# PSUM as one tile of eight banks, minima of the first heads one by one, and VectorE's attention work in program order, in a transformer block

## The chip, the cores and the metric

The kernel runs on one core of a Trainium2 chip. The metric is the device time of one execution in microseconds (us). Three executions took 3985.17, 3985.71 and 3986.91 us; the median is 3985.71 us. The engines are called PE (TensorE, matrix multiplications), ACT (ScalarE), DVE (VectorE), POOL (GpSimd) and SP (SyncE). PSUM is the accumulator memory that PE writes and that ACT and DVE read. Here it has 128 partitions and eight banks, each of 512 float32 numbers per partition.

## What is computed

Both parts work on h of shape (8, 1024, 512): causal attention with 16 heads of width 32, and a feed-forward part of width 2048. Each normalises its input, and its result is normalised again and added to the input.

```python
# attention, for x = layernorm(h)
qvk = (x @ Wqvk).reshape(b, s, 3, H, HD)
scores = einsum('bshi,bthi->bsth', q, k)
scores = (scores + mask) / sqrt(d)
...
h = h + layernorm(attention(layernorm(h)))
# feed-forward, for x = layernorm(h)
hidden = x @ W1 + b1
imag   = w_imag * sin(theta + hidden * 0.1)
hidden = hidden + (cos(theta) * w_real + sin(theta) * w_imag) * imag * 0.1
y = relu(hidden) @ W2 + b2
out = h + layernorm(y)
```

The lines above are a summary of the reference in its own names. All matmuls are in float32. In the trace each float32 matmul of 512 columns shows as two records.

## The kernel before

**The work and its order.** The kernel takes the eight batches one after the other. A batch has attention, in four groups of four heads (`attention`, L631), and then the feed-forward part (`feed_forward`, L743). Every PE instruction is pinned to program order: the helper `matmul` (L88) and `transpose_on_pe` (L94) call `keep_in_program_order`. Much of ACT's work is pinned too, through `in_order` (L91). DVE's instructions are not pinned, and a scheduler chooses their order before the program is built. Functions that are written as generators (`project_qkv`, `norm1`, `finish_block`) are advanced step by step between the other stages, so that their matmuls stand among those of the attention. SP issues the loads and stores.

**PSUM.** `psum` (L78) gives out four slots of up to two banks, s0 to s3, each with a tag of its own. `drained` (L84) puts a slot back at the end of a list, and the next request takes the one at its head. So a request for one bank takes a slot of two. Requests are: `pq` and `pv` (projections, one bank or half of one), `sc` (scores, two banks), `parts_t` (transposed maxima), `st` (transposed scores, two banks), `acc` (the weighted values in its first bank and, in the second half of the queries, the sums of weights in its second), `y` (output projection), `xn_t` (transposes of the normalised input), `ph` (two chunks of the hidden layer, one bank each) and `ys` (four row blocks of the result in two tiles of two).

**A group of heads.** `find_maxima` (L419) works through four runs, in the order of `MAX_RUNS` (L403). A run has one or two units. A unit (`run_unit`, L447) takes two tiles `sc`, one for heads 0 and 1 and one for heads 2 and 3, multiplies queries by keys for all four heads into them, and lets DVE take minima of each row (the sign is turned). Where a block of keys is visible as a whole, one `tensor_reduce` (L471) covers the two heads of a tile. On the diagonal a masking operation (L478) runs for each head, and leaves `es`, which ACT turns into exponentials (L497). After each run `MAX_FILL` (L412) steps of the next group's projections follow: `pq` (L359) with its copy L372, and `pv` (L377) with its copy L388. The maxima are split into parts (L431), transposed on PE (`transpose_maxima`, L528) and copied to `mT` (L533), by ACT for the first half of the queries and by DVE for the second.

`weigh` (L537) then runs for three units of keys in the first half and seven in the second (`KEY_UNITS`, L414). It fills two tiles `st`, ACT turns each into weights `w` (L573), and POOL cuts off what the mask hides (L577). The next unit's scores are issued ahead of the weighted values (`weighted_values`, L590) of this one. In the second half `add_weights` (L616, the addition is L621) sums the weights on DVE, `weight_sums` (L603) multiplies the total by ones, and `divide` (L623) has a logarithm, an exponential and a product (L626 to L628). These sums are put off into the first run of the next group. Two last units of maxima, `MAX_LATE`, run between the units of weights.

**The feed-forward part.** `hidden` (L752) takes a chunk of 128 hidden columns: four multiplications into one bank of `ph`, then ACT's `hid` (L770), then DVE's chain and ACT's sine. `accumulate` (L784) adds the chunk of two steps before into `ys`. A `ph` tile serves two chunks and is drained after the second. Between them stand steps of `finish_block` (L711): `y` with its copy L728, the residual addition (`residual_stages`, L259, the function `add`), and the transposes into `x2T` (L237). `end` (L797) reads `ys` with four additions (L802). `norm1` (L330) does the same for the input of the next batch, with its `scale` at L341 (`normalised`, L218).

Of the kernel before, what the change touches and what calls it, by code (L numbers as in the profile page):

```python
# [16 lines left out]
P = 128  # L17
# [14 lines left out]
def kernel(  # L32
# [42 lines left out]
    free_slots = list(range(4))  # L75
    slot_of = {}

    def psum(shape, name, dtype=F32):  # L78
        slot = free_slots.pop(0)
        t = ps.tile(shape, dtype, tag=f"s{slot}", name=name)  # L80
        slot_of[id(t)] = slot, t
        return t

    def drained(t):  # L84

        free_slots.append(slot_of.pop(id(t))[0])

    def matmul(*args, **kwargs):  # L88
        tc.keep_in_program_order(nc.tensor.matmul(*args, **kwargs))  # L89
# [90 lines left out]
    def prepare_parameters():  # L180

        pt = psum([P, 4 * NFC], "prm_t")
        transpose_on_pe(pt, prm_in, ident[: 4 * NFC, : 4 * NFC])
        nc.vector.tensor_copy(prm, pt)
        drained(pt)
        th, wr, wi = (prm[:, n * NFC : (n + 1) * NFC] for n in (1, 2, 3))
        sn = small.tile([P, NFC], F32, tag="sn", name="sn", bufs=1)
        cs = small.tile([P, NFC], F32, tag="cs", name="cs", bufs=1)
        kk = small.tile([P, NFC], F32, tag="kk", name="kk", bufs=2)
        reduce_angle(sn, kk, th, 0.0)  # L190
        clamp(sn)
        nc.scalar.activation(sn, sn, AF.Sin)
        kc = small.tile([P, NFC], F32, tag="kk", name="kc", bufs=2)
        reduce_angle(cs, kc, th, 0.25)
        nc.vector.tensor_scalar(cs, cs, math.pi / 2, None, ALU.add)
        clamp(cs)
        nc.scalar.activation(cs, cs, AF.Sin)
        nc.vector.tensor_mul(cs, cs, wr)
        nc.vector.tensor_mul(sn, sn, wi)
        nc.vector.tensor_add(cs, cs, sn)  # L200
        nc.vector.scalar_tensor_tensor(coef, cs, 0.1, wi, ALU.mult, ALU.mult)
# [16 lines left out]
    def normalised(dst, src, mv, rs):  # L218
        nc.vector.tensor_scalar(dst, src, mv[:, 0, 0:1], rs, ALU.subtract, ALU.mult)
# [13 lines left out]
    def transpose_rows(src, dst, evacuate):  # L233
        pt = psum([P, KC, P], "xn_t")
        for kc in range(KC):
            transpose_on_pe(pt[:, kc, :], src[:, kc * P : (kc + 1) * P], ident)
        evacuate(dst, pt)  # L237
        drained(pt)
# [20 lines left out]
    def residual_stages(target, y):  # L259
# [8 lines left out]
        def add(t):  # L268
            normalised(y(t), y(t), mvs[t], rss[t])
            nc.vector.tensor_add(target(t), target(t), y(t))  # L270
# [59 lines left out]
    def norm1(b):  # L330
# [10 lines left out]
        def scale(t):  # L341
            normalised(xs[t], xs[t], mvs[:, t : t + 1, :], rss[:, t : t + 1])
# [7 lines left out]
    def project_qkv(b, g):  # L350
# [7 lines left out]
        def queries_or_keys(n, half):  # L358
            pq = psum([P, HALF], "pq")  # L359
            c0 = 2 * n * D + g * P  # L360
            for kc in range(KC):
                matmul(
                    pq,
                    wqvk_sb[:, kc, c0 : c0 + P],
                    xnT[b, half][:, kc, :],
                    start=(kc == 0),
                    stop=(kc == KC - 1),
                )
                if kc == 1:
                    yield True  # L370
# [5 lines left out]
        def values(t0):  # L376
            pv = psum([P, 2, P], "pv")  # L377
            c0 = D + g * P
            for t in (t0, t0 + 1):
                for kc in range(KC):  # L380
                    matmul(
                        pv[:, t - t0, :],
                        xnT[b, t // TPB][:, kc, (t % TPB) * P : (t % TPB + 1) * P],
                        wqvk_sb[:, kc, c0 : c0 + P],
                        start=(kc == 0),
                        stop=(kc == KC - 1),
# [32 lines left out]
    def find_maxima(b, g, work, sums):  # L419
# [11 lines left out]
        def split(c):  # L431
# [6 lines left out]
            else:  # L438
                nc.vector.tensor_tensor(top, top, mxs[c][:, 1], ALU.min)
            parts = parts_q[c].rearrange("p i (j r) -> p i j r", r=HD)  # L440
            engine, keep = (nc.vector, id) if c else (nc.gpsimd, tc.keep_in_program_order)
            for r in range(MPART):
                keep(engine.tensor_copy(parts[:, :, :, r], top))
                if r < MPART - 1:
                    keep(engine.tensor_tensor(top, top, parts[:, :, :, r], ALU.subtract))

        def run_unit(pieces):  # L447

            scs = [psum([P, 2, HALF], "sc") for _ in range(HC)]
            at = 0  # L450
            placed, left = [], []
            for i, kc in pieces:
                k0 = kc * HALF
                n = min(HALF, (i + 1) * P - k0)
                for j in range(HPG):
                    r = slice(j * HD, (j + 1) * HD)
                    matmul(
                        scs[j // 2][:, j % 2, at : at + n],
                        t[r, 0, i * P : (i + 1) * P],
                        t[r, 1, k0 : k0 + n],  # L460
                        start=True,
                        stop=True,
# [3 lines left out]
            for k, sc in enumerate(scs):  # L466
                es = None
                for i, kc, cols, n in placed:
                    mx = mxs[i // TPB][:, kc, i % TPB, 2 * k : 2 * k + 2]
                    if kc < i // TPB:  # L470
                        nc.vector.tensor_reduce(  # L471
                            out=mx, in_=sc[:, :, cols], op=ALU.min, axis=mybir.AxisListType.X
                        )
# [3 lines left out]
                    for m in range(2):  # L477
                        nc.vector.tensor_tensor_reduce(  # L478
                            out=es[:, m, cols],
                            in0=sc[:, m, cols],  # L480
                            in1=mask[:, HALF - n :],
                            scale=1.0,
                            scalar=FMAX,
                            op0=ALU.add,
                            op1=ALU.min,
                            accum_out=mx[:, m : m + 1],
# [41 lines left out]
    def transpose_maxima(parts, evacuate):  # L528
        pt = psum([P, TPB, P], "parts_t", BF16)
# [7 lines left out]
    def weigh(b, g, c, keys, mT):  # L537
# [3 lines left out]
        sts = [psum([P, 2, HALF], "st") for _ in range(HC)]  # L541
        at = 0
        placed, own = [], []
        for kb in keys:
# [3 lines left out]
            for j in range(HPG):  # L548
                r = slice(j * HD, (j + 1) * HD)
                matmul(  # L550
                    sts[j // 2][:, j % 2, cols],
                    minus1[r, :],
                    mT[r, HALF - n :],
                    start=True,
                    stop=False,
                )
            for j in range(HPG):
                r = slice(j * HD, (j + 1) * HD)
                matmul(
                    sts[j // 2][:, j % 2, cols],  # L560
                    t[r, 1, kb * P : (kb + 1) * P],
                    t[r, 0, q0 : q0 + n],
                    start=False,
                    stop=True,
# [25 lines left out]
    def weighted_values(acc, b, g, first, last, weights, placed):  # L590

        for k, (kb, cols, n) in enumerate(placed):
            for j in range(HPG):
                r = slice(j * HD, (j + 1) * HD)
                matmul(
                    acc[r, 0, HALF - n :],
                    v[b, g][:, kb, r],
                    weights[j // 2][:, j % 2, cols],
                    start=first and k == 0,
                    stop=last and k == len(placed) - 1,  # L600
                )

    def weight_sums(acc, first, last, weights, placed):  # L603

        for k, (_, cols, n) in enumerate(placed):
            for j in range(HPG):
                r = slice(j * HD, (j + 1) * HD)
                matmul(
                    acc[r, 1, HALF - n :],
                    ones,  # L610
                    weights[j // 2][:, j % 2, cols],
                    start=first and k == 0,
                    stop=last and k == len(placed) - 1,
                )

    def add_weights(total, weights, placed):  # L616

        for t, w in zip(total, weights):
            for _, cols, n in placed:
                q = slice(HALF - n, HALF)  # L620
                nc.vector.tensor_add(t[:, :, q], t[:, :, q], w[:, :, cols])  # L621

    def divide(acc, dst):  # L623

        inverse = tmp.tile([P, HALF], F32, tag="tmp", name="inverse")
        in_order(nc.scalar.activation(inverse, acc[:, 1, :], AF.Ln))  # L626
        in_order(nc.scalar.activation(inverse, inverse, AF.Exp, scale=-1.0))
        nc.vector.tensor_tensor(dst, acc[:, 0, :], inverse, ALU.mult)  # L628
        drained(acc)

    def attention(b, wvT, after):  # L631
# [23 lines left out]
        for g in range(NG):  # L655
# [4 lines left out]
            for c in range(2):  # L660
# [3 lines left out]
                for u, keys in enumerate(units):  # L664
# [4 lines left out]
                    if at == 2:  # L669
                        mTs.append(transpose_maxima(parts_q[1], nc.vector.tensor_copy))  # L670
# [13 lines left out]
                    def step(accs=accs, u=u, last=u == len(units) - 1, weights=weights, c=c, g=g,  # L684
                             placed=placed, total=total, dst=wvT[c][:, g, :]):
                        if u == 0:
                            accs.append(psum([P, 1 + c, HALF], "acc"))
                        acc = accs[0]
                        weighted_values(acc, b, g, u == 0, last, weights, placed)
                        if last and c:  # L690

                            def whole():
                                weight_sums(acc, True, True, *total)
                                divide(acc, dst)

                            summing[0] = whole
                        elif last:
                            nc.scalar.copy(dst, acc[:, 0, :])
# [12 lines left out]
    def finish_block(b, half, wvT, x2T):  # L711
# [5 lines left out]
        def project(t):  # L717
            y = psum([P, D], "y")
            for kc in range(KC):
                matmul(  # L720
                    y,
                    wvT[:, kc, t * P : (t + 1) * P],
                    wo_sb[:, kc, :],
                    start=(kc == 0),
                    stop=(kc == KC - 1),
# [17 lines left out]
    def feed_forward(b, x2T, between):  # L743
# [6 lines left out]
        ys, hids, phs, us, ks = {}, {}, {}, {}, {}  # L750

        def hidden(c):  # L752

            half, fc = divmod(c, NFC)
            n, pair = c % 2, c // 2
            if n == 0:
                phs[pair] = psum([P, 2, HALF], "ph")
# [3 lines left out]
            ph, hid, u, k = (x[pair][:, n, :] for x in (phs, hids, us, ks))  # L761
            for kc in range(KC):
                matmul(
                    ph,
                    w1_sb[:, kc, fc * P : (fc + 1) * P],
                    x2T[half][:, kc, :],
                    start=(kc == 0),
                    stop=(kc == KC - 1),
                )
            nc.scalar.activation(hid, ph, AF.Identity, bias=prm[:, fc : fc + 1])  # L770
            if n:
                drained(phs[pair])
# [11 lines left out]
        def accumulate(c):  # L784
            half, fc = divmod(c, NFC)
            for t in range(TPB):
                if fc == 0 and t % 2 == 0:
                    ys[half, t // 2] = psum([P, 2, D], "ys")
                matmul(
                    ys[half, t // 2][:, t % 2, :],  # L790
                    hids[c // 2][:, c % 2, t * P : (t + 1) * P],
                    w2_sb[:, fc, :] if fc < NW2 else w2_tail[:, fc - NW2, :],
                    start=(fc == 0),
                    stop=(fc == NFC - 1),
                )

        def end(half):  # L797

            ybs = []
            for t in range(TPB):  # L800
                yb = tmp.tile([P, D], F32, tag="tmp", name="yb")
                nc.vector.tensor_add(yb, ys[half, t // 2][:, t % 2, :], b2_sb)  # L802
                if t % 2:
                    drained(ys[half, t // 2])
# [101 lines left out]
```

## Time and profile before

| | us |
|---|---|
| median of three executions | 3985.71 |
| the profiled execution's own time | 3986.48 |
| its span in the trace | 3984.8 |
| PE busy | 3826.0 (96% of the span) |
| DVE busy | 2767.8 (69%) |
| ACT busy | 1503.3 (38%) |
| POOL busy | 515.8 (13%) |
| mean granted clock of PE | 0.998 of full speed |

The profile comes from one execution. The page lists busy times, the granted clock of PE and the costliest groups of instructions; a group's row gives the line, the engine, the operation, the tiles written and read, the count, the busy time, the mean of one, and the idle time ahead of it with the instruction that ended most of it. A row of waits such as `PE pq L89 <- DVE mx L471` says that PE sat idle ahead of matmuls into `pq`, and that the last event before they started was the end of a minimum on DVE at line 471; three numbers follow, the sum in us, the number of times, and the longest. All matmuls are recorded at line 89, so they are told apart by the tile that they write. In the timeline each row has its start, its length, what it is, and in brackets the idle time before it with its releaser. A batch takes 492.6 us; its feed-forward part takes about 238.

### The profile page before, as it was taken

The page shows a single profiled execution, that of the slowest core. Times are in us where ns is not written, and L with a number is a line of the kernel's source. Part 1 is how long each engine was busy: PE and PEld are TensorE (multiplying, and loading weights), DVE is VectorE, ACT ScalarE, POOL GpSimd, SP SyncE. Part 2 cuts the span into 40 slices and gives each one's busy share as a digit, 9 for nine tenths or more (in the row PEclk, how much of TensorE's full clock was granted, in tenths as well). Part 3 has the DMA queues.
Part 4 walks back from the last instruction along what each step waited for, and adds up shares of the span by engine and source line. Part 5 has one row for each costly group of instructions (what it writes and reads, how often), then busy time and mean ns, then how long its engine had stood idle before and what let it go on. Part 6 is the DMA issues. An engine that isn't in the chain of part 4 may idle for free.

```text
span 3984.8 us, 51177 instructions
## 1 busy us (share of the span) xinstructions
PE 3826.0 (96%) x19457; PEld 1756.0 (44%) x19457; DVE 2767.8 (69%) x6033; ACT 1503.3 (38%) x2804; POOL 515.8 (13%) x1131
## 2 busy tenths in 40 slices
PE   8999999999999999999999999999999999999998
PEld 4444444444444444444444444444444444444343
DVE  4767767676766777667776677766767666677666
ACT  4552135521354214542145421454214542146321
POOL 1121011200112001120011200111001110011200
PEclk9999999999999999999999999999999999999999
DMA  4000000000000000000000000000000000000000
GB/s 151 25 19 22 22 30 9 17 21 21 30 14 12 22 21 32 12 12 21 22 32 12 12 21 21 33 12 11 22 22 33 12 11 0 22 22 12 1 8 14
DMA packets 43495, 86.42 MB, mean 22 GB/s; under 512 B 4144, under 2 KB 4208, under 8 KB 42736
## 3 DMA queue, kind: packets, MB, share of 16 engines
q1 hardware_dynamic: 39056, 71.61, 5.4%
q10 hardware_dynamic: 4192, 11.53, 0.7%
q8 instruction: 152, 2.49, 0.2%
q14 instruction: 95, 0.78, 0.1%
HBM read 66.36 MB, written 16.78 MB: 21 GB/s over the span
## 4 chain that ended last, share of the span: by engine, by line
PE 83%; DVE 10%; ACT 2%; issue 2%; POOL 1%; DMA 0%; POOLq 0%; ACTq 0%; SPq 0%
PE ph L89 22%; PE ys L89 22%; PE pq L89 11%; PE st L89 6%; PE pv L89 6%; PE acc L89 6%; PE sc L89 5%; PE y L89 4%; DVE mx L471 4%; ACT w L573 2%; DVE es L478 2%; DVE w L621 1%; DVE st L207 1%; PE xn_t L95 1%; DVE x L270 1%
## 5 line engine op out<-in xcount | busy, mean ns | idle before, releaser
L89 PE MATMUL ph<-x2T,w_sb 128*128 128x512 f32 x2048 | 921.1, 593 | 12.1 <-ACT hid L770 6.7
L89 PE MATMUL ys<-w_sb,hid 128*128 128x512 f32 x1536 | 691.0, 592 | 0.0
L573 ACT ACTIVATE w<-st 128x1024 f32<-128x1024 f32 (+1 forms) x640 | 565.8, 936 | 295.8 <-PE st L89 288.2
L89 PEld LDWEIGHTS ph<-x2T,w_sb 128*128 128x128 f32 x2048 | 385.3, 190 | 487.5 <-issue 466.8
L621 DVE TENSOR_TENSOR w<-w 128x1024 f32<-128x1024 f32 (+3 forms) x448 | 443.2, 1033 | 161.0 <-PE acc L89 108.0
L478 DVE CUSTOM_DVE_ANT_0 es<-sc,mask 128x128 f32<-128x128 f32 (+3 forms) x1024 | 433.5, 487 | 149.3 <-PE sc L89 149.3
L89 PE MATMUL pq<-xnT,wqvk_sb 128*128 128x512 f32 x1024 | 480.9, 609 | 43.0 <-DVE mx L471 43.0
L778 ACT ACTIVATE u<-u 128x512 f32<-128x512 f32 x256 | 161.1, 629 | 891.0 <-DVE u L178 890.9
L89 PEld LDWEIGHTS ys<-w_sb,hid 128*128 128x128 f32 x1536 | 291.2, 190 | 368.6 <-issue 344.2
L471 DVE TENSOR_REDUCE mx<-sc 128x2 f32<-128x1024 f32 x256 | 302.2, 1220 | 145.6 <-PE sc L89 145.6
L577 POOL TENSOR_SCALAR_AFFINE_SELECT w<-w 128x256 f32<-128x256 f32 x512 | 263.7, 534 | 729.4 <-ACT w L573 724.4
L89 PE MATMUL acc<-w,v 128*32 128x512 f32 (+3 forms) x3072 | 323.8, 495 | 25.0 <-POOL w L577 16.8
L770 ACT ACTIVATE hid<-ph,prm 128x512 f32<-128x512 f32 x256 | 175.2, 685 | 451.8 <-PE ph L89 451.8
L89 PE MATMUL st<-qk 32*128 32x512 f32 (+3 forms) x3072 | 334.7, 494 | 0.0
L89 PE MATMUL sc<-qk 32*128 32x512 f32 (+3 forms) x3072 | 312.8, 511 | 3.3 <-DVE mx L478 3.1
L781 DVE SCALAR_TENSOR_TENSOR hid<-u,coef,hid 128x512 f32<-128x512 f32 x256 | 192.2, 751 | 173.5 <-ACT u L778 173.5
L773 DVE TENSOR_SCALAR u<-hid,prm 128x512 f32<-128x512 f32 x256 | 123.8, 484 | 270.9 <-ACT hid L770 270.9
L89 PEld LDWEIGHTS pq<-xnT,wqvk_sb 128*128 128x128 f32 x1024 | 182.8, 190 | 289.8 <-issue 182.4
L497 ACT ACTIVATE es<-es,mx 128x512 f32<-128x512 f32 (+3 forms) x512 | 279.6, 550 | 1.9 <-DVE mx L478 1.9
L89 PE MATMUL pv<-wqvk_sb,xnT 128*128 128x128 f32 x2048 | 259.5, 280 | 13.5 <-DVE mx L478 13.5
L89 PEld LDWEIGHTS pv<-wqvk_sb,xnT 128*128 128x128 f32 x2048 | 239.0, 192 | 75.4 <-DVE mx L478 40.8
L89 PE MATMUL y<-wo_sb,wvT 128*128 128x512 f32 x512 | 233.5, 599 | 0.0
(96 smaller groups left out, 3380.1 us busy)
## 6 DMA issues: line engine op xcount, KB each, us to landing
xin<-in_L_attn_h_dram SPq DMA_DIRECT2D x112, 256.0 KB, 2.6
x<-in_L_attn_h_dram SPq DMA_DIRECT2D x64, 256.0 KB, 2.7
out_dram<-x SPq DMA_DIRECT2D x64, 256.0 KB, 2.0
w_tail<-in_L_ffn_W_dram SPq DMA_DIRECT2D x8, 1024.0 KB, 5.2
w_sb<-in_L_ffn_W_dram ACTq DMA_DIRECT2D x1, 4096.0 KB, 15.8
wqvk_sb<-in_L_attn_Wqvk_dram ACTq DMA_DIRECT2D x3, 1024.0 KB, 9.5
w_sb<-in_L_ffn_W_dram ACTq DMA_DIRECT2D x1, 3072.0 KB, 25.1
wo_sb<-in_L_attn_Wo_dram ACTq DMA_DIRECT2D x1, 1024.0 KB, 5.5
```

Source lines behind the costliest of these rows:

```text
L89: tc.keep_in_program_order(nc.tensor.matmul(*args, **kwargs))
L95: tc.keep_in_program_order(nc.tensor.transpose(*args))
L471: nc.vector.tensor_reduce(out=mx, in_=sc[:, :, cols], op=ALU.min, axis=mybir.AxisListType.X)
L478: nc.vector.tensor_tensor_reduce(out=es[:, m, cols], in0=sc[:, m, cols], in1=mask[:, HALF - n :], scale=1.0, scalar=FMAX, op0=ALU.add, op1 ...
L497: nc.scalar.activation(es[:, m, cols], es[:, m, cols], AF.Exp, bias=mx[:, m : m + 1], scale=-1.0, accum_out=row[:, m : m + 1],)
L573: in_order(nc.scalar.activation(w[:, :, :width], st[:, :, :width], AF.Exp, scale=-1.0))
L577: select = nc.gpsimd.affine_select(out=square, in_=square, compare_op=ALU.is_ge, fill=0.0, base=0, pattern=[[0, 2], [1, P]], channel_multi ...
L621: nc.vector.tensor_add(t[:, :, q], t[:, :, q], w[:, :, cols])
L770: nc.scalar.activation(hid, ph, AF.Identity, bias=prm[:, fc : fc + 1])
L773: nc.vector.tensor_scalar(u, hid, 0.1, prm[:, NFC + fc : NFC + fc + 1], ALU.mult, ALU.add)
L778: sine = nc.scalar.activation(u, u, AF.Sin)
L781: nc.vector.scalar_tensor_tensor(hid, u, coef[:, fc : fc + 1], hid, ALU.mult, ALU.add)
```

## The change

The change has three parts, and a change of form.

1. PSUM becomes one tile `banks` of eight banks. `psum` gives out one bank, or two neighbouring ones, as a view of this tile: among the free places it takes the one whose last bank to be drained was drained longest ago in program order. `drained` can mark one bank of a pair. Requests that need one bank get one: `pq`, `pv`, `y`, `ph`, `ys`, `xn_t`, `parts_t`, the parameters, and `acc`. The sums of the weights get a bank of their own, `whole_sum`, which is drained after the logarithm. Only `sc` and `st` ask for pairs.
2. In a unit with full keys the minimum of the first tile (k = 0) is taken head by head, with two reductions in place of one. The second tile keeps one reduction for two heads.
3. DVE's work in attention is pinned to program order: the minima, the split of the maxima, the copy of `mT`, the additions of weights, the product of the division, the residual additions and the scaling in `norm1`. The casts and the chain in `hidden`, the moments and the additions in `end` are not pinned.
4. The helper `matmul` goes, and its calls are written as `in_order(nc.tensor.matmul(...))`. PE's order stays the program's.

The core of the diff:

```diff
-    free_slots = list(range(4))
-    slot_of = {}
-
-    def psum(shape, name, dtype=F32):
-        slot = free_slots.pop(0)
-        t = ps.tile(shape, dtype, tag=f"s{slot}", name=name)
-        slot_of[id(t)] = slot, t
+    banks = ps.tile([P, 8, HALF], F32, name="banks")
+    done_at = [0] * 8
+    clock = [0]
+    banks_of = {}
+
+    def psum(shape, dtype=F32):
+        size = math.prod(shape[1:]) * (2 if dtype == BF16 else 4)
+        n = -(-size // (4 * HALF))
+        free = [k for k in range(9 - n) if None not in done_at[k : k + n]]
+        k = min(free, key=lambda k: max(done_at[k : k + n]))
+        t = banks[:, k : k + n, :].rearrange("p b n -> p (b n)")[:, : size // 4]
...
+        done_at[k : k + n] = [None] * n
+        banks_of[id(t)] = list(range(k, k + n)), t
         return t
-    def drained(t):
-
-        free_slots.append(slot_of.pop(id(t))[0])
+    def drained(t, n=None):
+
+        mine = banks_of[id(t)][0]
+        for k in [mine[0]] if n is None and len(mine) == 1 else mine if n is None else [mine[n]]:
+            clock[0] += 1
+            done_at[k] = clock[0]
...
         def add(t):
-            normalised(y(t), y(t), mvs[t], rss[t])
-            nc.vector.tensor_add(target(t), target(t), y(t))
+            in_order(normalised(y(t), y(t), mvs[t], rss[t]))
+            in_order(nc.vector.tensor_add(target(t), target(t), y(t)))
...
-            scs = [psum([P, 2, HALF], "sc") for _ in range(HC)]
+            scs = [psum([P, 2, HALF]) for _ in range(HC)]
...
                     if kc < i // TPB:
-                        nc.vector.tensor_reduce(
-                            out=mx, in_=sc[:, :, cols], op=ALU.min, axis=mybir.AxisListType.X
-                        )
+
+                        for m in [slice(0, 2)] if k else [slice(0, 1), slice(1, 2)]:
+                            in_order(
+                                nc.vector.tensor_reduce(
+                                    out=mx[:, m],
+                                    in_=sc[:, m, cols],
+                                    op=ALU.min,
+                                    axis=mybir.AxisListType.X,
+                                )
+                            )
                         continue
...
-                nc.vector.tensor_add(t[:, :, q], t[:, :, q], w[:, :, cols])
+                in_order(nc.vector.tensor_add(t[:, :, q], t[:, :, q], w[:, :, cols]))
...
-    def divide(acc, dst):
+    def divide(acc, total, dst):
 
         inverse = tmp.tile([P, HALF], F32, tag="tmp", name="inverse")
-        in_order(nc.scalar.activation(inverse, acc[:, 1, :], AF.Ln))
+        in_order(nc.scalar.activation(inverse, total, AF.Ln))
+        drained(total)
         in_order(nc.scalar.activation(inverse, inverse, AF.Exp, scale=-1.0))
-        nc.vector.tensor_tensor(dst, acc[:, 0, :], inverse, ALU.mult)
+        in_order(nc.vector.tensor_tensor(dst, acc, inverse, ALU.mult))
         drained(acc)
...
-                        mTs.append(transpose_maxima(parts_q[1], nc.vector.tensor_copy))
+                        mTs.append(
+                            transpose_maxima(
+                                parts_q[1], lambda *a: in_order(nc.vector.tensor_copy(*a))
+                            )
+                        )
...
-                            accs.append(psum([P, 1 + c, HALF], "acc"))
+                            accs.append(psum([P, HALF]))
...
-                                weight_sums(acc, True, True, *total)
-                                divide(acc, dst)
+                                whole_sum = psum([P, HALF])
+                                weight_sums(whole_sum, *total)
+                                divide(acc, whole_sum, dst)
...
+            ph = psum([P, HALF])
             if n == 0:
-                phs[pair] = psum([P, 2, HALF], "ph")
...
             nc.scalar.activation(hid, ph, AF.Identity, bias=prm[:, fc : fc + 1])
-            if n:
-                drained(phs[pair])
+            drained(ph)
...
-                if fc == 0 and t % 2 == 0:
-                    ys[half, t // 2] = psum([P, 2, D], "ys")
+                if fc == 0:
+                    ys[half, t] = psum([P, D])
```

## The prediction

> **What bounds the kernel now.** I read the table of busy time first, then what TensorE (PE) waits for, then the timeline of single spots, then the granted clock.
>
> ```profile
> PE 3826.0 (96%) x19457; PEld 1756.0 (44%) x19457; DVE 2767.8 (69%) x6033; ACT 1503.3 (38%) x2804; POOL 515.8 (13%) x1131
> ```
>
> PE is busy for 96% of the span, so the kernel is a stream of matmuls, and every other engine lies beside it. What is left over is in PE's waits (us in total, times, longest):
>
> ```profile
> PE pq L89 <- DVE mx L471: 43.0, 86, 2.8
> PE xn_t L95 <- DVE xn L219: 18.8, 9, 17.2
> PE acc L89 <- POOL w L577: 16.8, 26, 1.0
> PE pv L89 <- DVE mx L478: 13.5, 31, 0.4
> PE st L89 <- DVE mT L533: 12.3, 7, 1.8
> ...
> PE acc L89 <- DVE mx L471: 8.2, 31, 0.3
> PE ph L89 <- ACT hid L770: 6.7, 8, 0.8
> ```
>
> The rows of the whole view, without the start-up row xn_t, sum to 124.9 us, 15.6 per batch. That is all a better handing out of PSUM could win. The row that decides my forecast is the last: `ph` waits eight times, once per batch, for ScalarE's (ACT's) read `hid`. Here is one of the eight:
>
> ```profile
> 1783.94 1.02 PE L89 MATMUL ph<-x2T,w_sb 128*128 128x512 f32 x2
> 1785.07 0.69 ACT L770 ACTIVATE hid<-ph,prm 128x512 f32<-128x512 f32 x1 [3.32 <-PE ph L89]
> ...
> 1785.81 1.12 PE L89 MATMUL ph<-x2T,w_sb 128*128 128x512 f32 x2 [0.84 <-ACT hid L770]
> ```
>
> The matmuls at 1783.94 are the last of chunk 0, into the first bank of a two-bank tile. Those at 1785.81 are the first of chunk 1, into the *second* bank, which nobody has touched. They need nothing of `hid`, yet they start when its read of the *first* bank ends. So in this program a write into one bank of a PSUM tile waits for the earlier read of another bank of the same tile: waits go by tile, not by bank. In the steady state nothing shows, because work on another tile stands between:
>
> ```profile
> 1799.72 3.60 PE L89 MATMUL ph<-x2T,w_sb 128*128 128x512 f32 x8
> 1803.15 3.60 PE L89 MATMUL ys<-w_sb,hid 128*128 128x512 f32 x8
> ```
>
> In this stretch ACT reads `ph` from 1803.35 for 0.69 us, beside `ys`. The four slots of L78 are four tiles, and that lets PE write one while another is read.
>
> **The change part by part.** *One tile of eight banks.* With waits by tile, everything in PSUM is one object: a matmul into any bank waits for each read traced before it, and each read waits for the matmuls traced before it. PE and the readers then take turns. The price of a turn is read from the spot above. The matmuls of chunk 0 start 0.43 apart, so the next was due at 1784.80; it started at 1785.81, and that pair took 1.12 instead of 1.02 us. The loss is 1.01 + 0.10 = 1.11 us: the reader's 0.69 plus **0.42** for the two handovers. (Bounds of the 0.42: nothing, if the handovers are hidden elsewhere, and 0.84, the whole idle time of that row, which would add 182 turns x 0.42 x 8 = 611 us to what follows.)
>
> Readers per group of four heads (32 groups), from the groups of instructions:
> - causal minima L478: 433.5/32 = 13.5 us, in 5 units of scores
> - full-key minima L471: 302.2/32 = 9.4, in 4 units, plus the split of the next part, 0.6
> - exponentials of the weights L573: 565.8/32 = 17.7, in 10 units
> - copies of queries and keys L372, 76.4/32 = 2.4 in 4; of values L388, 47.6/32 = 1.5 in 4; transposed maxima L533, 0.58 + 0.42 = 1.0 in 2; first half's result L698, 0.6 in 1
> - the division, L626, L627, L628 one after another: 0.60 + 0.63 + 0.69 = 1.9 in 1
>
> This is 48.6 us and 31 turns: 48.6 + 31 x 0.42 = 61.6 per group, 246.5 per batch. Per batch there are also 8 transposes of the next input (0.59 + 0.42: 8.1), 8 output projections and 8 transposes behind them (0.58 + 0.42: 16.0), 32 hidden chunks (0.69 + 0.42: 35.5) and 8 reads of `ys` in two rows (8 x 0.68 + 2 x 0.42: 6.3). The sum is 312.4 per batch. Today's 15.6 of idle are waits of the same kind and go into it: 296.8 more. Times 8 is 2374; the last batch has no next input and no projections for it, -15. **Added: about 2360 us**, on 3986.5 us (the profiled execution's own time, 0.8 above the median shown): 6346. With turns at nothing it is (312.4 - 182 turns x 0.42 - 15.6) x 8 = 1763, so 5750.
>
> *The clock.* PE would now pause some 31 times per group. The granted clock in before already falls at sparse places:
>
> ```profile
> 3676.42:3679.84 3.42, 2.89 (x20) 1.24 (x20) 3.42 (x7) 2.31 (x8) 0.00 (x0) 1.00 0.00 0
> 3679.84:3683.25 3.41, 2.27 (x20) 1.12 (x20) 3.41 (x17) 2.40 (x9) 0.22 (x1) 1.00 0.00 0
> 3683.25:3686.67 3.42, 2.71 (x16) 1.27 (x12) 3.42 (x15) 0.59 (x1) 1.21 (x5) 0.50 0.00 0
> 3686.67:3690.08 3.41, 3.41 (x20) 1.78 (x18) 3.39 (x12) 0.09 (x1) 0.00 (x0) 0.50 0.02 5
> ```
>
> (The second column is PE's busy time, the third from the end the clock.) After a stretch of 3.41 us with PE busy for 2.27, the next ran at 0.50, although other stretches with 1.66 to 2.20 were not followed by one. Serialized, a group is about 53.4 us of PE work in some 111, so 1.64 of 3.41. All of the attention at half clock would add its PE work once more, 53.4 x 32 = 1709 us; none adds nothing. I take a third, since the rows show both answers: **+570**, in all **6900**. The feed-forward part stays dense (two times 3.43 us of matmuls for every 1.11 us lost).
> [...]
> [...]
>
> *Single banks, and who gets them.* The sums of weights get their own bank, `ph`, `ys` and the accumulator one each, and the least recently drained bank is given. Under waits by tile this moves nothing: which bank is given doesn't matter.
>
> *First heads one by one.* 128 pair reductions of 1.22 us become 256 of half the width. A half isn't in the trace: it takes from 0.61 (half the pair) to 0.69 (a 512-wide pass, L207), so the split costs 0 to 0.16 each, 0 to 20 us of VectorE in all. I take 0.16 (the row of the same width). Beside PE it is hidden by VectorE's 31% of idle time; in turns it is on the path, and is in the sum.
>
> *VectorE in program order.* The instructions and their count stay. What goes: the copy of the transposed maxima (L533) that today stands behind a residual addition is traced ahead of it, so the 12.3 us row goes in 7 batches. What could come: minima queued behind additions of weights (L621, 1.03 us each, two per unit). Under turns these run while ACT reads and PE writes, so I cost both at nothing beyond the sum; without that cover it would be 14 additions per group, up to 14.4 x 32 = 461 us, which the upper end takes in. The scalar and GpSimd work is not moved, nor any DMA.
>
> **Rivals.**
> *Waits by bank, and the change does what it seems to be built for.* The pq row (43.0), pv (13.5), acc behind minima (8.2), mT (12.3) and st behind `xnT` (3.2) go: -80, **3906**. For it: in these rows a projection that needs one bank waits for a slot of two, both banks of which must be read first. Against it: the `ph` row.
> *Waits by bank, but pairs are broken up by singles.* Single banks for `pq` leave no free adjacent pair but the one just read. By the grant rule the second unit of the third run gets the banks of the same run's first heads and waits about 1.1 us, and the first weights get the banks of the late minima (0.9, a third unit 0.15); two pq waits of 0.45 go: +1.25 per group, 5.0 per batch, less 1.5 for the mT row: +28, **4014**. It decides where the single bank lies inside the oldest pair.
> *Faster than forecast but still in turns.* Handovers at nothing and no half clock: 5750.
> For the forecast the other side is the first rival: one mechanism (a guard by bank), worth 80 us, deciding as soon as a write to one bank doesn't wait for another bank's read.
>
> **How the numbers follow.** Waits by tile, in turns: 0.88, since all eight places of this kind in the trace show it. Waits by bank with the gain: 0.05, faster. Broken pairs: 0.05, slower. Between the two, within 0.2% (about what a measurement of this kernel can tell from no change): 0.02. The range for the turns goes from 5800 (5750 with cheap handovers, a little clock loss) to 8000 (6346 and 1709 of clock are 8055; with queued additions still more); I give what lies outside 0.07. So 5800 to 8000 holds about 8 in 10. Slower 0.93, same 0.02, faster 0.05.
>
> **What would show it.** In the changed profile PE's share falls to near 60%; the waits name rows like ys behind ACT `hid`, some 30 per batch, and pq behind any reader, each about the reader's time plus 0.3; ACT and VectorE wait for PE in turn; windows of attention show 0.50 clocks. Feed-forward takes about 280 us per batch instead of 238, attention over 500 instead of 255. Wrong it is if ys starts while `hid` still reads, with `ph` in another bank: then a rival holds, and the time is below 4050. Only the clock is wrong if all stretches show 1.00 and the time is near 6350.

## The result and the profile after

The changed kernel takes **4028.21 us** (median of four executions, 4027.42 to 4028.94), against 3986.31 us for the kernel before on the same chip: a ratio of 1.0104, 95% interval 1.0086 to 1.0121. It is 1% slower, the forecast was 6900 us, and of the rivals the one with broken pairs (4014) is the nearest. The profiled execution has a span of 4026.5 us against 3984.8 of before, 41.7 more.

The table of busy time of the changed kernel:

```profile
PE 3889.7 (97%) x19457; PEld 1780.9 (44%) x19457; DVE 2791.0 (69%) x6161; ACT 1508.6 (37%) x2804; POOL 545.7 (14%) x1131
```

PE's share did not fall; PE is busy for 63.7 us *more* than before, with the same matmuls. PE's waits in the changed kernel (all of PSUM is one tile, so all are called `banks`, and the lines tell them apart: 373 is `pq`, 394 `pv`, 472 `sc`, 576 and 587 `st`, 625 the weighted values, 640 the sums of weights, 805 `ph`, 832 `ys`):

```profile
PE banks L576 <- DVE mx L502: 21.1, 46, 0.6
PE banks L625 <- POOL w L606: 18.0, 34, 0.7
PE banks L472 <- DVE mx L490: 17.6, 38, 3.4
...
PE banks L640 <- DVE w L654: 11.4, 7, 1.6
PE banks L576 <- ACT w L602: 9.2, 40, 0.5
PE banks L832 <- DVE hid L824: 9.0, 8, 1.1
PE banks L576 <- DVE mx L490: 8.8, 25, 0.4
```

Set against the rows of before: pq (43.0), pv (13.5), mT (12.3) and acc behind minima (8.2) are gone, as the first rival said. The row of `ph` behind `hid` (6.7) is gone too, and with it my forecast: `ph` no longer waits for a read of another bank. In the steady state `ys` starts while `hid` still reads `ph` in another bank of the same tile, which was my sign of being wrong:

```profile
1824.42 3.60 PE L832 MATMUL banks<-w_sb,hid 128*128 128x512 f32 x8
1824.63 0.69 ACT L813 ACTIVATE hid<-banks,prm 128x512 f32<-128x512 f32 x1 [2.85 <-PE banks L805]
```

Other rows have come, for scores (L472) and transposed scores (L576), which take pairs. And the scores show a loss that is mostly in no row of waits. Their group, first of the kernel before, then of the changed kernel:

```profile
L89 PE MATMUL sc<-qk 32*128 32x512 f32 (+3 forms) x3072 | 312.8, 511 | 3.3 <-DVE mx L478 3.1
```
```profile
L472 PE MATMUL banks<-qk 32*128 32x512 f32 (+3 forms) x3072 | 368.7, 519 | 18.2 <-DVE mx L490 17.6
```

3072 matmuls of the same mean length (511 and 519 ns) cover 312.8 us in one and 368.7 us in the other. In the kernel before the records of a unit's four heads lie beside each other: one after another, 3072 of 511 ns would take 1570 us, and in batch 3 four of them start within 0.02 us, from 1537.84 on. In the changed kernel the banks of two heads come free later than those of the other two in some runs. There the records of the later two heads come behind the others, and PE is busy for longer with the same work: 3.28 us instead of 2.00 in the third run of the first group in batch 3. Here it is on PE, of the kernel before:

```profile
1537.84 2.00 PE L89 MATMUL sc<-qk 32*128 32x512 f32 x24
1540.29 1.12 PE L89 MATMUL pq<-xnT,wqvk_sb 128*128 128x512 f32 x2 [0.45 <-DVE mx L471]
```

and on PE and DVE of the changed kernel:

```profile
1553.35 1.56 PE L472 MATMUL banks<-qk 32*128 32x512 f32 x12
1555.25 1.72 PE L472 MATMUL banks<-qk 32*128 32x256 f32 x12 [0.34 <-DVE mx L490]
1556.90 0.70 PE L373 MATMUL banks<-xnT,wqvk_sb 128*128 128x512 f32 x1
```
```profile
1554.51 2.42 DVE L490 TENSOR_REDUCE mx<-banks 128x1 f32<-128x512 f32 x3 [0.70 <-PE banks L472]
```

Before, the 24 records take 2.00 us in one piece, and `pq` then waits 0.45. After, `pq` doesn't wait, but the 24 records come as 12 and 12, with 0.34 us between, and the second twelve begin at 1555.25, just behind the first half reduction that started at 1554.51. The run lasts 3.56 instead of 2.45 us.

PE's order is the same in both kernels, so its records can be set side by side one by one. The difference in start grows or shrinks at these places (us per batch, mean of batches 1 to 6; g0 to g3 are the groups of heads):

| place | what happens | per batch |
|---|---|---|
| third run of each group (+1.10 x 4), second and fourth run of g3 (+1.10, +0.51) | second pair of the unit's heads comes late | +6.0 |
| first transposed scores (+1.03 in g0 and g3, +0.42 in g1 and g2) | the same | +2.9 |
| second and fourth run of g0 to g2 (-0.51 to -0.74) | `pq` no longer waits for a whole slot | -3.4 |
| later transposed scores and values of g0 to g3 | bits of both signs | about -1.4 |
| g0: behind the transposed maxima | `mT` is in time | -1.8 |
| g0: last scores and sums (+0.70, +1.70, +0.59) | the sums wait for the last additions | +3.0 |
| sum | | +5.3 |

Times eight this is 42, the difference in span.

### The profile page after: what moved, and what is told of

It is laid out like the page before. It is cut to its first block, busy times and chain, and to the rows that moved or that the text cites. A ratio compares the mean times of both kernels' runs of the same rounds, so it can differ in the third digit from the quotient of the medians.

```text
span 4026.5 us, 51219 instructions
## 1 busy us (share of the span) xinstructions
PE 3889.7 (97%) x19457; PEld 1780.9 (44%) x19457; DVE 2791.0 (69%) x6161; ACT 1508.6 (37%) x2804; POOL 545.7 (14%) x1131
## 4 chain that ended last, share of the span: by engine, by line
PE 85%; DVE 10%; ACT 2%; POOL 2%; issue 1%; DMA 0%; POOLq 0%; SPq 0%; DVEq 0%; ACTq 0%
PE banks L832 22%; PE banks L805 21%; PE banks L373 11%; PE banks L472 8%; PE banks L394 6%; PE banks L587 4%; PE banks L760 4%; PE banks L625 4%; DVE w L654 3%; DVE mx L490 3%; PE banks L576 2%; PE banks L105 2%; ACT w L602 1%; PE banks L640 1%; DVE es L502 1%
## 5 line engine op out<-in xcount | busy, mean ns | idle before, releaser
L805 PE MATMUL banks<-x2T,w_sb 128*128 128x512 f32 x2048 | 918.9, 593 | 5.4 <-ACT x2T L247 5.4
L832 PE MATMUL banks<-w_sb,hid 128*128 128x512 f32 x1536 | 691.3, 593 | 9.0 <-DVE hid L824 9.0
L602 ACT ACTIVATE w<-banks 128x1024 f32<-128x1024 f32 (+1 forms) x640 | 567.1, 940 | 307.1 <-PE banks L587 233.0
L805 PEld LDWEIGHTS banks<-x2T,w_sb 128*128 128x128 f32 x2048 | 386.0, 190 | 478.0 <-issue 468.7
L654 DVE TENSOR_TENSOR w<-w 128x1024 f32<-128x1024 f32 (+2 forms) x448 | 444.4, 1031 | 200.3 <-PE banks L625 123.4
L502 DVE CUSTOM_DVE_ANT_0 es<-banks,mask 128x128 f32<-128x128 f32 (+3 forms) x1024 | 432.8, 488 | 128.9 <-PE banks L472 128.9
L373 PE MATMUL banks<-xnT,wqvk_sb 128*128 128x512 f32 x1024 | 480.6, 609 | 0.0
L490 DVE TENSOR_REDUCE mx<-banks 128x1 f32<-128x512 f32 (+1 forms) x384 | 309.9, 863 | 217.4 <-PE banks L472 217.4
L472 PE MATMUL banks<-qk 32*128 32x512 f32 (+3 forms) x3072 | 368.7, 519 | 18.2 <-DVE mx L490 17.6
L625 PE MATMUL banks<-w,v 128*32 128x512 f32 (+3 forms) x3072 | 329.0, 496 | 18.6 <-POOL w L606 18.0
L587 PE MATMUL banks<-qk 32*128 32x512 f32 (+3 forms) x3072 | 336.2, 496 | 0.0
L472 PEld LDWEIGHTS banks<-qk 32*128 32x128 f32 x3072 | 161.7, 185 | 168.8 <-issue 68.6
```

Of the source, the lines that this page charges most:

```text
L373: nc.tensor.matmul(pq, wqvk_sb[:, kc, c0 : c0 + P], xnT[b, half][:, kc, :], start=(kc == 0), stop=(kc == KC - 1),)
L472: nc.tensor.matmul(scs[j // 2][:, j % 2, at : at + n], t[r, 0, i * P : (i + 1) * P], t[r, 1, k0 : k0 + n], start=True, stop=True,)
L490: nc.vector.tensor_reduce(out=mx[:, m], in_=sc[:, m, cols], op=ALU.min, axis=mybir.AxisListType.X,)
L502: nc.vector.tensor_tensor_reduce(out=es[:, m, cols], in0=sc[:, m, cols], in1=mask[:, HALF - n :], scale=1.0, scalar=FMAX, op0=ALU.add, op1 ...
L587: nc.tensor.matmul(sts[j // 2][:, j % 2, cols], t[r, 1, kb * P : (kb + 1) * P], t[r, 0, q0 : q0 + n], start=False, stop=True,)
L602: in_order(nc.scalar.activation(w[:, :, :width], st[:, :, :width], AF.Exp, scale=-1.0))
```

## The experiments

Two theories stood at the start. A: waits go by bank, and the loss is that single banks break up pairs. B: the loss is DVE's program order. And a question stood for the step of my forecast that fell: is a tile of eight banks guarded by bank and a smaller one as a whole, or is there no such difference?

**Aligned pairs.** One expression of the changed kernel is different:

```diff
-        free = [k for k in range(9 - n) if None not in done_at[k : k + n]]
+        free = [k for k in range(0, 9 - n, n) if None not in done_at[k : k + n]]
```

> The changed kernel, with pairs given out only at banks 0-1, 2-3, 4-5 and 6-7; nothing else differs. Theory A (waits go by bank, and the loss is pairs broken up by single banks): the 1.10 us ahead of the second unit of the third run of each group (4.4 per batch), the 1.6 us in the runs of the last group and most of the 3 us around the first weights go, 8 to 11 us per batch, so 3940 to 3965 us. Theory B (the loss is VectorE's work in program order): nothing of this depends on where pairs lie, so 4020 to 4035.

Measured: 3916.39 us, ratio to the kernel before 0.9826 (0.9811 to 0.9840), below the range of A. B is refuted as the main cause: only the rule for the place of the pairs differs, and it is worth 112 us. The second, third and fourth runs of every group now gain 0.52 us or more, and none of them loses. On PE the third run of the same group and what follows it:

```profile
1509.05 2.00 PE L472 MATMUL banks<-qk 32*128 32x512 f32 x24
1510.98 3.70 PE L373 MATMUL banks<-xnT,wqvk_sb 128*128 128x512 f32 x8
```

The 24 records are one piece again, and `pq` follows at once. The group of the scores is back near the 312.8 us of the kernel before:

```profile
L472 PE MATMUL banks<-qk 32*128 32x512 f32 (+3 forms) x3072 | 314.5, 513 | 0.3 <-DVE mx L502 0.2
```

PE is busy for 3813.3 us, 76 less than in the changed kernel. I had counted 8 to 11 us per batch and got 14.5, since I left out that the runs which lost 1.10 now *win* 0.52, as the others do.

**DVE left to the scheduler.** In the changed kernel, each `in_order` around an instruction of DVE is taken away:

```diff
-            in_order(normalised(y(t), y(t), mvs[t], rss[t]))
-            in_order(nc.vector.tensor_add(target(t), target(t), y(t)))
+            as_scheduled(normalised(y(t), y(t), mvs[t], rss[t]))
+            as_scheduled(nc.vector.tensor_add(target(t), target(t), y(t)))
```

(and so for the minima, the split, the copy of `mT`, the additions of weights, the product and the scaling; `as_scheduled` does nothing.)

> The changed kernel with VectorE's attention work left to the scheduler, as in the kernel before. Theory A: the order is worth about 0.5 us per batch either way (a gain of 1.8 at the transposed maxima of the first group against a loss of 3.0 at its end, and a gain of about 1.7 in the third group), so 4020 to 4040. Theory B: the loss goes, 3980 to 3995.

Measured: 4043.16 us, 1.0140 (1.0123 to 1.0157), 3 us above A's range and slower than with the order, so B is out. What is lost against the changed kernel lies in one place, once per batch: 2.7 and 4.4 us in turn from batch to batch, of which the first group gives 1.1 back. In the third group the scheduler puts three scalings of the next input between the reductions. On DVE (lines stand four further down than in the changed kernel):

```profile
673.64 1.29 DVE L494 TENSOR_REDUCE mx<-banks 128x1 f32<-128x512 f32 x2
674.85 1.45 DVE L232 TENSOR_SCALAR xin<-xin,mva,rsa 128x512 f32<-128x512 f32 x3
676.22 1.22 DVE L494 TENSOR_REDUCE mx<-banks 128x2 f32<-128x1024 f32 x1
```

The reads of that run end later, PE's third run stretches (4.60 us to the start of `pq`, against 3.56 for the same run of the changed kernel), and then the clock falls from 1.00 to 0.50. Stretches of 3.41 us, with PE's busy time second and the clock third from the end:

```profile
679.41:682.82 3.41, 3.04 (x17) 1.64 (x18) 3.41 (x7) 2.15 (x7) 0.00 (x0) 1.00 0.02 7
682.82:686.23 3.41, 3.41 (x5) 1.33 (x6) 2.60 (x16) 0.00 (x0) 0.00 (x0) 0.50 0.00 0
686.23:689.65 3.42, 3.42 (x29) 1.62 (x27) 0.52 (x1) 1.57 (x6) 0.00 (x0) 1.00 0.00 0
```

Set against the kernel before, that run costs 2.40 per batch and the `pq` behind it, at half clock, 2.26. So the program order doesn't cost the changed kernel its time; with broken pairs it keeps reads that PE waits for from being delayed (4028 us with it, 4043 without).

**The order alone**, in the kernel before, with its slots and its reduction for two heads. The edit wraps the same instructions in `in_order`:

```diff
-            normalised(y(t), y(t), mvs[t], rss[t])
-            nc.vector.tensor_add(target(t), target(t), y(t))
+            in_order(normalised(y(t), y(t), mvs[t], rss[t]))
+            in_order(nc.vector.tensor_add(target(t), target(t), y(t)))
```

> The kernel before, with its four slots and one reduction for two heads, and only VectorE's attention work pinned to program order. Theory A: 3975 to 3992; the wait of the transposed maxima (12.3 us) goes, a wait of the sums of weights for the last additions comes (about as much). Theory B: 4015 to 4030.

Measured: 3996.82 us, 1.0026 (1.0016 to 1.0037): 11 us slower, a little outside A's range and far from B's. The row of mT is gone and another has come:

```profile
PE acc L89 <- DVE w L625: 11.8, 7, 2.0
```

Record by record the first group wins 1.8 us behind the maxima and loses 3.0 at its end (4.8 in one batch). What is late there: the four residual additions of the block before now stand one by one between the additions of weights. In the changed kernel the last six additions of weights on DVE, and the sums of weights on PE:

```profile
1600.15 0.77 DVE L280 TENSOR_TENSOR x<-x,yb 128x512 f32<-128x512 f32 x1
1600.85 4.28 DVE L654 TENSOR_TENSOR w<-w 128x768 f32<-128x768 f32 x6
```
```profile
1604.58 1.65 PE L640 MATMUL banks<-w,ones 128*32 128x512 f32 x8 [1.63 <-DVE w L654]
```

**Two tiles of four banks**, in place of one of eight:

```diff
-    banks = ps.tile([P, 8, HALF], F32, name="banks")
+    banks = [ps.tile([P, 4, HALF], F32, tag=f"b{h}", name="banks") for h in range(2)]
...
-        free = [k for k in range(9 - n) if None not in done_at[k : k + n]]
+        free = [k for k in range(9 - n) if None not in done_at[k : k + n] and k // 4 == (k + n - 1) // 4]
...
-        t = banks[:, k : k + n, :].rearrange("p b n -> p (b n)")[:, : size // 4]
+        t = banks[k // 4][:, k % 4 : k % 4 + n, :].rearrange("p b n -> p (b n)")[:, : size // 4]
```

> The changed kernel with PSUM as two tiles of four banks in place of one of eight; a pair lies within one tile. If only the tile of eight is guarded by bank, and a smaller tile as a whole (as the row of ph behind hid in the kernel before says of a tile of two), PE and the readers take turns within each tile: with two tiles about half of the turns I had priced at 1763 to 2360 us stay, so 4700 to 5400 us. If waits go by bank in every tile, 4020 to 4080, since only the places of the pairs differ.

Measured: 5634.06 us (one execution), above the first range and far from the second. Its busy times and some of PE's waits:

```profile
PE 4323.2 (77%) x19457; PEld 1900.5 (34%) x19457; DVE 2803.4 (50%) x6161; ACT 1521.5 (27%) x2804; POOL 507.2 (9%) x1131
```
```profile
PE banks L625 <- ACT w L602: 222.1, 153, 2.4
PE banks L373 <- DVE mx L502: 179.9, 70, 2.9
...
PE banks L832 <- ACT hid L813: 70.0, 89, 1.1
```

This is the kind of profile that I had predicted for the change: `ys` waits behind `hid` up to 1.1 us, and the mean granted clock is 0.904. The clock records of before and after hold two speeds, 1.00 and 0.50. If this run has no others, 0.904 means that about 19% of its 5632 us were at half speed, which is an estimate. The grants of L80 say in which of the two tiles each bank lies. Of the 240 times that `ys` follows a `ph`, its first row block lies in the tile of `ph` 88 times, in another bank, and waits for `hid` every time; it lies in the other tile 152 times and never waits. So in these counts a tile of four is guarded as a whole, as the tile of two is in the eight `ph` waits of before, and turns cost more than I had priced (5634 us, priced at 5400 at most); but the tile of eight isn't guarded so, as the `ys` at 1824.42 beside the read at 1824.63 shows.

**The old slots in one tile of eight.** The kernel before, with each slot a view of one tile; order and sizes stay:

```diff
+    banks = ps.tile([P, 8, HALF], F32, name="banks")
...
-        t = ps.tile(shape, dtype, tag=f"s{slot}", name=name)
+        t = banks[:, 2 * slot : 2 * slot + 2, :].rearrange("p b n -> p (b n)")[:, : size // 4]
```

(with the views for bfloat16 and for three dimensions as in the change.)

> The kernel before, with its four slots of two banks given out in the same order, but as views of one tile of eight banks; nothing else. If the tile of eight is guarded by bank and a tile of two as a whole: the wait of ph for hid (6.7 us) goes, and those that wait for a read of the second bank of a slot, pv behind the causal minima (13.5) and a few us of the others; the wait of pq (43.0) stays, since one reduction reads both banks: 3955 to 3972. If a tile of eight is guarded as a whole: over 5700. If tiles make no difference: 3984 to 3990.

Measured: 3972.77 us, 0.9966 (0.9954 to 0.9978), 0.8 us above the end of the first range. The guard of the one tile is worth 14 us by itself (3986.65 before on the same chip). The wait of `ph` is gone, but `ys` then waits for the end of DVE's chain on the chunk that it reads (1.1 us, 8 times), and nothing is won there. What is won are the waits of `pv`, 0.50 in each group behind the first transposed scores. The group of `pv` in the kernel before, and then `pv` and `pq` in this one, where both are called `banks`:

```profile
L89 PE MATMUL pv<-wqvk_sb,xnT 128*128 128x128 f32 x2048 | 259.5, 280 | 13.5 <-DVE mx L478 13.5
```
```profile
L95 PE MATMUL banks<-wqvk_sb,xnT 128*128 128x128 f32 x2048 | 259.5, 280 | 0.0
L95 PE MATMUL banks<-xnT,wqvk_sb 128*128 128x512 f32 x1024 | 480.9, 609 | 47.3 <-DVE mx L477 47.3
```

`pv` waited for a read of the second bank of its slot, and doesn't any more; `pq` still waits, since one reduction reads both banks. All three are as the first case said.

**The split.** Two runs: aligned pairs with one reduction for the first two heads, and the kernel before with the split alone.

```diff
-                        for m in [slice(0, 2)] if k else [slice(0, 1), slice(1, 2)]:
+                        for m in [slice(0, 2)]:
```

> Aligned pairs, with the first tile's two heads again under one reduction of 1.22 us. Theory A (a projection that takes the first bank can start when that bank alone has been read, and this is what the split buys): the 0.53 us in each of twelve runs per batch come back, 51 us, so 3960 to 3972. Theory D (the grant of banks alone is enough, the split buys nothing): 3905 to 3920.

Measured: 3964.5 us, 0.9947 (0.9932 to 0.9961), 48 us slower than with the split; A holds. The row of `pq` is back:

```profile
PE banks L373 <- DVE mx L490: 46.1, 93, 3.2
```

In the kernel before, with the loop of the change around `tensor_reduce`:

> The kernel before, with slots of two banks, and only the split of the first tile's reduction. Theory A: a slot is free only when both its banks are read, so the split buys nothing, and two halves take 0.07 us longer than the pair, at some 90 waits: 3985 to 3995. Theory D': the split helps by itself: below 3978.

Measured: 3999.49 us, 1.0034 (1.0020 to 1.0047): the split alone costs 13 us. Its row of `pq` grows from 43.0 to 56.7; each of twelve runs in a batch is 0.16 us longer. DVE itself has only 8.3 us more in reductions (384 of them in 310.5 us, against 256 in 302.2), but they lie ahead of the first slot's release (two halves of 686 ns on average, against 1220 for the pair). So here the split paid only where a bank could be taken singly: 48 us won there, 13 lost in whole slots.

**Aligned pairs with DVE left to the scheduler** (both edits above together).

> Aligned pairs, with VectorE's attention work left to the scheduler. Theory A (the two parts add up: single banks in aligned pairs are worth about 10.6 us per batch, the order costs about 1.3 per batch): 3986 - 85 = 3901, so 3895 to 3907. Theory C (the order is needed for the single banks to pay): 3925 to 3960.

Measured: 3913.12 us, 0.9818 (0.9801 to 0.9834), between the two ranges. With aligned pairs the order matters little: 3.3 us from 3916.39, which the two intervals don't tell apart, and neither the 15 that it cost to drop it with broken pairs nor the 11 that it cost by itself. C falls.

**The residual additions early.** With aligned pairs, the first group's residual additions together, at the first unit of the second half:

```diff
                     if at >= first:
-                        advance(more)
+                        advance(more, 5 if g == 0 and at == first else 1)
```

> Aligned pairs and program order as in the aligned kernel, but in the first group the four residual additions of the block before are issued together at the first unit of the second half, into VectorE's 5 us without work behind the copy of the transposed maxima, and not one by one between the additions of weights. Theory A (those additions push the last additions of weights back, and the sums of weights and the next scores wait for them, 3.0 us in each of seven batches): 3916 - 21 = 3895, so 3890 to 3900. If the late additions are not what the sums wait for: 3914 to 3920.

Measured: 3908.57 us, 0.9806 (0.9791 to 0.9821), between the two ranges. The sums no longer wait, but mT does again (12.7 us, 7 times), though its copy is traced ahead. On DVE:

```profile
1533.14 0.69 DVE L280 TENSOR_TENSOR x<-x,yb 128x512 f32<-128x512 f32 x1
1533.74 0.42 DVE L706 COPY mT<-banks 128x512 bf16<-128x512 bf16 x1
1534.07 0.68 DVE L280 TENSOR_TENSOR x<-x,yb 128x512 f32<-128x512 f32 x1
```

So two pinned instructions ran against the order in which they were traced. I read it so: the pin of an instruction holds it behind the one traced just before it on its engine. Here that is a measurement of the residual, which is not pinned and runs early, so nothing holds the addition behind the copy. No run shows this rule alone. The next one follows it, and traces the measurements ahead of the transposed maxima and the additions directly behind the copy:

```diff
+            def together():
+                for stage in (measure, add):
+                    for t in range(TPB):
+                        stage(t)
+                    yield True
+                for t in range(TPB):
+                    store(t)
+                    yield True
...
-                return rest, len(KEY_UNITS[0])
+                return rest, 1
```

> Aligned pairs, with the first group's four residual additions traced directly behind the copy of the transposed maxima, so that each is pinned behind it (in the run before, their pins hung on measurements that were free to move, and the copy was late again). Theory A: both waits go, that of the transposed maxima and that of the sums of weights: about 3.0 us less in each of seven batches than with aligned pairs alone, 3892 to 3899. If only one of the two can be had: 3905 to 3916.

Measured: **3902.08 us**, 0.9787 (0.9774 to 0.9801), the fastest kernel of this study, again between the two ranges. Both waits are gone; 14 of the 21 us came. In the first group the transposed scores and values behind the copy now lose about 1.0 per batch, and the wait for POOL's selection rises from 17.9 to 25.3 us:

```profile
PE banks L625 <- POOL w L606: 25.3, 41, 1.0
```

Why the selections are later there was not tried.

## Why the prediction was wrong

**The step that failed** is the reading of the `ph` row: "waits go by tile, not by bank". The row says it of a tile of *two* banks, and for a tile of four it holds as well (5634 us). I carried it over to a tile of eight, which no row showed, and gave it 0.88. The tile of eight is guarded by bank in the runs: `ys` doesn't wait for the read of `ph` (1824.42 beside 1824.63), and putting the old slots into one such tile takes away the rows of `ph` (6.7) and `pv` (13.5). (A guard finer than a bank would fit the rows as well.) With this step the 2360 us of turns and the 570 us of clock fell. Why the guards differ is open. Sizes of two, four and eight were seen, but the tile of eight was also the only PSUM tile of its program and was asked for without a tag, where those of two and four had one; no run tells these three apart.

**The price of turns** was not wrong in kind: where they arise, PE's share falls to 77%, the waits are those that I named, and the mean granted clock is 0.904, by the estimate above half speed for a fifth of the time. In size it was low: two tiles of four were to take 4700 to 5400 us by it, and took 5634.

**Single banks.** "Which bank is given doesn't matter" fell with the first step: it matters most, 112 us between 4028 and 3916. The rival's place was right (the second unit of the third run waits for the same run's first heads, 1.1 us), the sign too. It put +1.25 on each group alike; it missed the second and fourth run of the last group (+1.10, +0.51) and the late sums of weights in the first (+3.0). It said +28 us; it was +42.

**First heads one by one.** DVE pays 8.3 us in reductions, inside my 0 to 20. I wrote that the split is in the sum of the turns, but the 302.2 us there are those of the kernel before, so it stood at nothing; in whole slots it costs 13 us. Where they go by bank it is worth 48 us.

**Program order.** That mT's wait goes was right (-1.8 in seven batches). That nothing else comes was wrong: the residual additions push the additions of weights back and the sums wait, +3.0. I had named minima behind additions as what could come, and not the sums. The range's low end, 5800, left both rivals out, which I had given 0.10 together.

## What to carry to other kernels

A row that shows a wait tells the rule for the object that it shows; before a forecast rests on it for another size or shape, look for a row of that size, or keep the other reading at its full chance. When buffers are given out singly and in pairs, ask which pair a single splits: 112 us lay in the step of one range. Where the four heads' score matmuls ran beside each other here, banks that came free one after another stretched the work more than the row of waits showed (56 us of busy time beside a row of 17.6), so compare the busy time of equal counts too.

## What the runs showed that I had not expected

The same 3072 score matmuls kept PE busy for 312.8 us with buffers that come free together and for 368.7 with buffers that come free in two halves, at nearly the same length of each.

PE's share of busy time didn't say when the clock falls: a stretch of 3.41 us with 3.04 busy was followed by half clock in one kernel, while one with 1.66 (1563.58 to 1566.99) was not in the kernel before. In the first of these, the changed kernel with DVE left to the scheduler, the mean granted clock was 0.992, against 0.997 with the order, and the fall shown above cost 1.7 us on one projection (8 records of `pq` in 5.40 instead of 3.70 us).

POOL's selections took 593 ns on average in the changed kernel and 534 in the kernel before; all POOL work was 545.7 us in the changed kernel and 515.8 before. This was not followed up.
